# A recurrent layer with a mixture of experts: the second phase's weight sums on VectorE, its additions in DMAs, and a strided down projection

## The chip, the cores and the metric

The kernel runs on one core of one Trainium2 chip. Its engines work side by side and wait for each other through semaphores: TensorE (PE in the profile; its weight loads are PEld), VectorE (DVE), ScalarE (ACT), GpSimd (POOL) and SyncE (SP). SyncE and GpSimd also issue the transfers (DMAs). The metric is the time of one execution on the device in microseconds (us); lower is better. The kernel before takes 4173.52 us (median of 3 runs, 4172.38 to 4174.35).

## What is computed

Eight sequences of 1024 tokens, 512 numbers each (8192 tokens in all), in f32. `_L0_attn_ref` is a gated recurrence with an output projection, `_L0_ffn_ref` a mixture of 32 experts, of which each token uses the best one, beside a shared expert:

```python
x = L0_attn_x
xn = _layernorm(x, axis=-1)
s = _L0_attn_ref(xn, W1, b1, W2, b2, init_h)   # ... out_h @ W2 + b2
g = _silu(_L0_ffn_ref(xn, gate_w, ...))        # shared_out + routed_out
x = x + s * g
```

For a routed token, scaled by its gate's sigmoid, the expert computes `silu(x @ gate) * (x @ up) @ down`; gate and up are 512 x 1024 per expert, down is 1024 x 512.

## The kernel before

**First phase.** 16 chunks of 512 tokens. For each chunk the input projections of the recurrence and of the shared expert are computed, in a seven-product form of block multiplication (Strassen-Winograd: the products P1 to P7 of sums of blocks, in place of eight plain products). The order of all engines is written out by hand in slots. Beside it, one chunk later, `project_out` (from L1166) computes the two output projections of a chunk, called halves: half 0 is `out_h @ W2`, half 1 the shared expert's down projection. Each half has seven products of 8 matmul calls in two PSUM banks, `chain` and `side`. Copies on ScalarE (L1180, L1209, L1217) and additions on VectorE (L1203, L1214) and GpSimd (L1210) bring them into two SBUF tiles, which `out_store` (L1161) writes to `rec2`, a table in device memory with three parts per token: x (copied there by `keep`, L598), the recurrence's output, and the shared expert's output. The normalized, scaled tokens go to `rec1`. The router's choice becomes lists of tokens per expert.

**Second phase.** The experts are taken in order of their number of tokens; the place e has room for `WIDTHS[e]` tokens (376 down to 224), what does not fit goes to a loop at the end (none does here). A `Chunk` is one expert with its tokens, in up to three tiles of 128. Its first stage (gate and up) runs in `strassen` for the places 1 to 27 (width 240 and more) and in `plain` for 0 and 28 to 31. `strassen` has four steps p of seven products each: P1, P5, P2, P6, a down group, P3, P7, a down group, P4. A down group (`down`, L307) multiplies one block of 128 hidden rows by the down weights into four PSUM accumulators; each f32 matmul call shows as two matmuls in the profile, so a group is eight. Down groups run behind: the last two of an expert run in step 0 of the next one. Results of a product are taken from PSUM by ScalarE copies (L384) and VectorE additions (L396, L404 and L406); SiLU on ScalarE and products on VectorE (L408, L413, L416) give the hidden rows. P7 and P4 share a bank: L406 must have read it before P4 is added into it.

The sums of weight blocks that the seven products need are made in `weight_sum` (L213), for each half q of an expert's columns: S3 and S1 on GpSimd (L219, L221), S2 and S4 on VectorE (L223, L225). Each works on 128 x 1024 numbers.

**From the accumulators to the output.** After an expert's last down group, four VectorE transposes in 32 x 32 blocks (L330) read the accumulators into `yT`. `store` writes it to a buffer in device memory by four DMAs on SP (L431), `fetch` reads it back as rows of tokens by up to three DMAs on SP (L440). `gather_rest` (L269) brings the tokens' three parts from `rec2`. Then, for each tile t: `bias` adds b2 (L470), `sums` adds the expert's result to the shared one (L460), `silu` on ScalarE (L465), `finish` multiplies by the recurrence's output and adds x (L478, L479) and scatters the rows to the output by an indirect DMA on GpSimd (L480). The last expert (`direct`) has no store and fetch; TensorE transposes its result (L453).

**The order.** Nothing schedules the second phase: instructions stand on each engine in the order of the calls. A loop (from L1633) puts steps into lists, `between[j]` for the hidden block j of 8; those of an even j run after P6 and the first down group of step p = j / 2, those of an odd j at the end of the step. GpSimd's and SP's queues also work in order: an instruction that waits holds what stands behind it. `alloc2` (L504) sets how many buffers a kind of tile has.

Of the kernel before, what the change touches and what calls it, by code (L numbers as in the profile page):

```python
# [17 lines left out]
P = 128  # L18
# [16 lines left out]
def tile_kernel(  # L35
# [70 lines left out]
    rec1 = dram.tile([N + 1, H], FP, name="rec1")  # L106
    rec2 = dram.tile([N + 1, 3 * H], FP, name="rec2")

# [62 lines left out]
    class Chunk:  # L171
# [41 lines left out]
        def weight_sum(self, q, name):  # L213
            if name == "S3":
                self.sm.append(self.alloc([P, 3, 2 * KQ, QW // 2], "sm", f"{self.name}_sm{q}"))
            s = self.sm[q].rearrange("p s c (b f) -> p s c b f", f=P)
            A11, A12, A21, A22 = (self.quarter(q, a, m) for m in range(2) for a in range(2))
            if name == "S3":
                nc.gpsimd.tensor_tensor(s[:, 1], A11, A21, ALU.subtract)  # L219
            elif name == "S1":  # L220
                nc.gpsimd.tensor_tensor(A21, A21, A22, ALU.add)  # L221
            elif name == "S2":
                nc.vector.tensor_tensor(s[:, 0], A21, A11, ALU.subtract)  # L223
            else:
                nc.vector.tensor_tensor(s[:, 2], A12, s[:, 0], ALU.subtract)  # L225
# [39 lines left out]
        def gather_rest(self):  # L265
            self.rest = []
            for t, n in self.tiles:
                r = self.alloc([P, 3 * H], "rest", f"{self.name}_rest{t}")
# [38 lines left out]
        def down(self, j, h):  # L307
            W = self.width
            for m in range(KH):
                nc.tensor.matmul(  # L310
                    accs[m][:, :W], lhsT=self.wd[:, j, m * P : (m + 1) * P], rhs=h[:, :W],
                    start=(j == 0), stop=(j == NI - 1),
                )
            if j == NI - 1:
                self.evict()

        def evict(self):
            W = self.width
            if self.direct:
                self.yT = self.alloc([P, KH, C], "yT", f"{self.name}_yT")  # L320
                for m in range(KH):
                    if m % 2:
                        nc.vector.tensor_copy(self.yT[:, m, :W], accs[m][:, :W])
                    else:
                        nc.scalar.copy(self.yT[:, m, :W], accs[m][:, :W])
                return
            nb = -(-W // BL)
            self.yT = self.alloc([P, C // BL, KH, BL], "yT", f"{self.name}_yT")
            for m in range(KH):
                nc.vector.transpose(  # L330
                    self.yT[:, :nb, m, :],
                    accs[m][:, : nb * BL].rearrange("p (b c) -> p b c", c=BL),
                )
# [91 lines left out]
        def store(self):  # L425
# [4 lines left out]
            for a in range(NA):  # L430
                nc.sync.dma_start(  # L431
                    out=rows[a, :, :nb, :],
                    in_=self.yT[a * BL : (a + 1) * BL, :nb].rearrange("p b m r -> p b (m r)"),
                )

        def fetch(self):
            rows, self.y = self.y, []
            for t, n in self.tiles:
                y = self.alloc([P, H], "y", f"{self.name}_y{t}")
                nc.sync.dma_start(out=y[:n, :], in_=rows[t * P : t * P + n, :])  # L440
                self.y.append(y)

        def sums(self, t):
# [3 lines left out]
            n = self.tiles[t][1]  # L447
            name, alloc, r = self.name, self.alloc, self.rest[t]
            z = r[:n, 2 * H :]
            if self.direct:  # L450
                y = bank(f"{name}_tb{t}")
                for m in range(KH):
                    nc.tensor.transpose(  # L453
                        y[:n, m * P : (m + 1) * P], self.yT[:, m, t * P : t * P + n], ident
                    )
                nc.vector.tensor_tensor(z, y[:n, :], z, ALU.add)
            else:
                zv = z.rearrange("p (m a r) -> p m a r", a=NA, r=BL)
                y = self.y[t][:n, :].rearrange("p (a m r) -> p m a r", a=NA, r=BL)
                nc.vector.tensor_tensor(zv, y, zv, ALU.add)  # L460

        def silu(self, t):
            if t < len(self.tiles):
                z = self.rest[t][: self.tiles[t][1], 2 * H :]
                nc.scalar.activation(z, z, AF.Silu)  # L465

        def bias(self, t):
            if t < len(self.tiles):
                n, r = self.tiles[t][1], self.rest[t]
                nc.vector.tensor_tensor(r[:n, H : 2 * H], r[:n, H : 2 * H], b2b[:n, :], ALU.add)  # L470

        def finish(self, t):

            if t >= len(self.tiles):
                return
            n, col, r = self.tiles[t][1], self.cols(t), self.rest[t]
            o = r[:n, H : 2 * H]
            nc.vector.tensor_tensor(o, o, r[:n, 2 * H :], ALU.mult)  # L478
            nc.vector.tensor_tensor(o, o, r[:n, :H], ALU.add)  # L479
            store = nc.gpsimd.indirect_dma_start(  # L480
                out=of[:, :], out_offset=bass.IndirectOffsetOnAxis(ap=col[:n, :], axis=0),
                in_=o, in_offset=None, bounds_check=N - 1, oob_is_err=False,
            )

# [82 lines left out]
    class Prep:  # L567
# [173 lines left out]
    def zero_rows():  # L741
# [5 lines left out]
        nc.gpsimd.dma_start(out=rec1[N : N + 1, :], in_=zrow)  # L747
        for q in range(3):
            nc.gpsimd.dma_start(out=rec2[N : N + 1, q * H : (q + 1) * H], in_=zrow)
# [411 lines left out]
    def out_store(c, half, m, o):  # L1161
        i = (c * NT + 2 * m) * P
        rows = rec2[i : i + 2 * P, (half + 1) * H : (half + 2) * H]
        nc.sync.dma_start(out=rows.rearrange("(q p) f -> p q f", p=P), in_=o)

    def project_out():  # L1166

        for n, u in enumerate(units):
# [8 lines left out]

            def evict(name, ps):
                t = part[name] = op.tile([P, 2, HC], FP, tag="e" + name[0], name=f"{name}_{n}")
                nc.scalar.copy(t, ps)  # L1180

            for name in UNIT:
                w = out_w.pop((u, name))
                ps = side if name in ("P2", "P5", "P3") else chain
                for q in range(2):
                    for p in range(NP):
# [12 lines left out]
                        if q == 1 and p == NP - 1:  # L1199
                            if name == "P1":  # L1200
                                evict("a1", ps)
                            elif name == "P2":
                                nc.vector.tensor_tensor(o[0][:, :, :HC], ps, part["a1"], ALU.add)  # L1203
                            elif name == "P6":
                                evict("a2", ps)
                            elif name == "P5":
                                evict("b5", ps)
                            elif name == "P7":
# [7 lines left out]
                            else:  # L1216
                                nc.scalar.copy(o[1][:, :, :HC], ps)  # L1217
                                at(now + 2, out_store, c, half, 1, o[1])
# [407 lines left out]
    with ExitStack() as c3:  # L1626
# [6 lines left out]
        for e, chunk in enumerate(chunks):  # L1633
            between = {j: [] for j in range(NI)}
            ahead = chunks[e + 1] if e + 1 < E else None
            if chunk.split:
                for j, name in ((0, "S3"), (0, "S1"), (2, "S2"), (3, "S4")):
                    between[j].append(lambda name=name: chunk.weight_sum(1, name))
            if e > 1:
                between[0].append(lambda: chunks[e - 2].finish(2))  # L1640
            if e:
                before = chunks[e - 1]
                between[1] += [before.store, before.fetch]
                for t in range(CT):
                    between[3].append(lambda t=t: before.bias(t))
# [22 lines left out]
            if e == E - 1:  # L1668
                between[7].append(lambda: before.finish(2))
                for t in range(CT):  # L1670
                    between[6].append(lambda t=t: chunk.bias(t))
            chunk.compute(pend, between)
# [9 lines left out]
    with tc.tile_pool(name="wo", bufs=3) as wo, tc.tile_pool(name="so", bufs=3) as so:  # L1682
# [4 lines left out]
        with tc.For_i(0, n, 1) as i:  # L1687
# [22 lines left out]
            for t in range(CT):  # L1710
                chunk.bias(t)
                chunk.sums(t)
# [34 lines left out]
```

## Time and profile before

| | us |
|---|---|
| median of 3 runs | 4173.52 |
| the profiled execution | 4176.65 |
| its span, first to last instruction | 4174.5 |
| first phase (to the first expert's matmul) | 2796 |
| second phase (to the last down matmul) | 1359 |
| PE busy | 4112.1 (99%) |
| DVE busy | 2371.7 (57%) |
| ACT busy | 2151.8 (52%) |
| POOL busy | 1428.3 (34%) |

The groups of instructions that the change touches, with count and mean duration:

| line, engine | what | count | mean |
|---|---|---|---|
| L219, POOL | weight sum S3 | 54 | 2367 ns |
| L221, POOL | weight sum S1 | 54 | 2400 ns |
| L223, L225, DVE | weight sums S2, S4 | 54 each | 1222, 1218 ns |
| L470, DVE | bias, tiles of 128 tokens | 54 | 679 ns |
| L460, DVE | result added, tiles of 128 | 53 | 678 ns |
| L478, L479, DVE | product, x added, tiles of 128 | 54 each | 665, 692 ns |
| L310, PE | down matmuls | 2048 | 396 ns |
| L480, POOL | scatters to the output | 84 | 1202 ns |

A bar of a matmul includes the time in which its results leave the array, so bars overlap; how far apart they start tells the rate. The times in a timeline are counted from the start of the span. "idle before" names what an engine waited for.

### The profile page before, as it was taken

The numbers are of one execution on the slowest core, as the hardware profiler recorded it, in microseconds if no ns is written. First come the engines' busy times: TensorE is split into PE (matmuls) and PEld (weight loads), VectorE is DVE, ScalarE is ACT, GpSimd is POOL, SyncE is SP. The second block draws the span as 40 slices with busy tenths as digits, with TensorE's granted clock in tenths as the row PEclk, the third lists the DMA queues.
The fourth block names the chain that finished last, engine by engine and source line by source line (L and its number), as shares of the span: only waits on it lengthen the run. The fifth ranks groups of instructions, "written<-read, shape, count | busy, mean of one in ns | idle before, by whom it ended". The sixth has DMA issues, their size and how long they took to land. (4 is left out here: it accounts for less than half of the span.)

```text
span 4174.5 us, 60006 instructions
## 1 busy us (share of the span) xinstructions
PE 4112.1 (99%) x21515; PEld 3637.9 (87%) x21515; DVE 2371.7 (57%) x3760; ACT 2151.8 (52%) x4095; POOL 1428.3 (34%) x1310
## 2 busy tenths in 40 slices
PE   7999999999999999999999999999999999999998
PEld 5788888888888888888888888877889999899998
DVE  6655544554545545455455555434676777777742
ACT  5667666766767667666676666631222222222211
POOL 5222111221122212212222113643556656565531
PEclk9999999999999999999999999999999999999999
DMA  7666666666666666657666665575667777677784
GB/s 255 234 223 219 212 220 204 217 222 215 220 206 202 229 220 216 215 198 232 211 216 215 209 211 190 181 245 179 222 224 248 245 245 251 240 256 252 256 271 145
DMA packets 567694, 926.13 MB, mean 222 GB/s; under 512 B 41469, under 2 KB 328093, under 8 KB 567394
## 3 DMA queue, kind: packets, MB, share of 16 engines
q1 hardware_dynamic: 539810, 832.29, 60.4%
q0 software_dynamic: 27584, 89.98, 6.5%
q8 instruction: 172, 2.82, 0.3%
q14 instruction: 128, 1.05, 0.1%
HBM read 805.27 MB, written 134.92 MB: 225 GB/s over the span
## 5 line engine op out<-in xcount | busy, mean ns | idle before, releaser
L894 PE MATMUL b<-t,sums 128*128 128x256 f32 x2536 | 652.2, 380 | 3.4 <-ACT u L908 1.8
L1191 PE MATMUL u<-wP,s 128*128 128x256 f32 x2032 | 596.3, 379 | 2.8 <-issue 2.8
L894 PEld LDWEIGHTS b<-t,sums 128*128 128x128 f32 x2536 | 480.7, 190 | 71.7 <-ACT u L908 3.0
L310 PE MATMUL acc<-e_h,e_wd 128*128 128x296 f32 (+15 forms) x2048 | 518.0, 396 | 0.0
L1191 PEld LDWEIGHTS u<-wP,s 128*128 128x128 f32 x2032 | 385.7, 190 | 57.2 <-issue 5.0
L310 PEld LDWEIGHTS acc<-e_h,e_wd 128*128 128x128 f32 x2048 | 374.2, 190 | 67.0
L894 PE MATMUL c<-xnT,sums 128*128 128x256 f32 x1268 | 327.0, 380 | 13.0 <-ACT p L908 11.6
L894 PE MATMUL c<-t,sums 128*128 128x256 f32 x1268 | 326.5, 380 | 4.2 <-ACT a L908 4.2
L894 PE MATMUL b<-xnT,nat 128*128 128x256 f32 x1268 | 326.3, 380 | 0.0
L894 PE MATMUL a<-xnT,nat 128*128 128x256 f32 x1268 | 325.7, 379 | 0.3
L894 PE MATMUL b<-t,nat 128*128 128x256 f32 x1268 | 325.4, 379 | 0.0
L259 POOL DMA_INDIRECT e_xs<-rec,fours x276 | 278.8, 1010 | 94.0 <-issue 81.6
L894 PEld LDWEIGHTS c<-xnT,sums 128*128 128x128 f32 x1268 | 240.5, 190 | 48.9 <-issue 9.3
L894 PEld LDWEIGHTS c<-t,sums 128*128 128x128 f32 x1268 | 241.2, 190 | 37.7 <-issue 4.9
L910 ACT ACTIVATE u<-b,vec 128x256 f32<-128x256 f32 x378 | 180.5, 478 | 178.1 <-PE b L894 178.1
L894 PEld LDWEIGHTS b<-xnT,nat 128*128 128x128 f32 x1268 | 241.5, 190 | 33.5 <-issue 0.5
L894 PEld LDWEIGHTS a<-xnT,nat 128*128 128x128 f32 x1268 | 240.6, 190 | 34.0 <-ACT c L908 1.5
L894 PEld LDWEIGHTS b<-t,nat 128*128 128x128 f32 x1268 | 241.1, 190 | 32.9
L480 POOL DMA_INDIRECT out_dram<-e_rest,idx x84 | 100.9, 1202 | 455.4 <-DVE e_rest L479 425.2
L972 DVE TENSOR_TENSOR d<-d,m 128x1024 f32<-128x1024 f32 x64 | 87.5, 1367 | 255.7 <-ACT m L968 255.7
L1191 PE MATMUL u<-wP,h 128*128 128x256 f32 x768 | 225.2, 379 | 0.0
L1191 PE MATMUL u<-wP,sh 128*128 128x256 f32 x720 | 215.6, 381 | 0.0
(288 smaller groups left out, 7998.2 us busy)
## 6 DMA issues: line engine op xcount, KB each, us to landing
sums<-sdram SPq DMA_DIRECT2D x300, 512.0 KB, 4.7
nat<-in_L_attn_W_dram SPq DMA_DIRECT2D x192, 512.0 KB, 4.3
e_w<-L_ffn_routed_gate_w_dram SPq DMA_DIRECT2D x128, 512.0 KB, 9.8
e_w<-n_L_ffn_routed_up_w_dram SPq DMA_DIRECT2D x128, 512.0 KB, 11.8
e_wd<-L_ffn_routed_down_w_dram SPq DMA_DIRECT2D x32, 2048.0 KB, 8.6
wP<-tdram SPq DMA_DIRECT2D x127, 512.0 KB, 3.7
nat<-L_ffn_shared_gate_w_dram SPq DMA_DIRECT2D x64, 512.0 KB, 4.4
nat<-n_L_ffn_shared_up_w_dram SPq DMA_DIRECT2D x64, 512.0 KB, 4.1
```

Of the source, the lines that this page charges most:

```text
L259: nc.gpsimd.indirect_dma_start(out=r[:, b, :], out_offset=None, in_=rec1.rearrange("n (a d) -> (n a) d", a=NA), in_offset=bass.IndirectOff ...
L310: nc.tensor.matmul(accs[m][:, :W], lhsT=self.wd[:, j, m * P : (m + 1) * P], rhs=h[:, :W], start=(j == 0), stop=(j == NI - 1),)
L480: store = nc.gpsimd.indirect_dma_start(out=of[:, :], out_offset=bass.IndirectOffsetOnAxis(ap=col[:n, :], axis=0), in_=o, in_offset=None, b ...
L894: nc.tensor.matmul(ps, lhsT=lhs[:, k, :], rhs=rhs[:, k, :], start=(new and k == 0), stop=(k == KQ - 1),  skip_group_check=True,)
L910: nc.scalar.activation(o, ps, AF.Identity, bias=bias(n, block))
L972: nc.vector.tensor_tensor(d, d, self.li, ALU.subtract)
L1191: nc.tensor.matmul(ps[:, q, :], lhsT=lhs[:, q * P : (q + 1) * P], rhs=w[:, p, :],  start=(q == 0 and p == 0 and name in ("P1", "P2", "P5") ...
```

## The change

It has five parts, all but one of them in the second phase.

- The weight sums S3 and S1 move from GpSimd to VectorE, and their places in the order move: for the expert that follows, S3 at j = 4, S1 at j = 5, S2 and S4 at j = 7; for the second half of the current one, S3 and S1 at j = 0, S2 and S4 at j = 2.
- The down weights of accumulator m are every fourth column from m on, where they were a block of 128 columns. `yT` holds the four numbers of a token's row next to each other, so the transposes write at a step of four numbers, and the rows in device memory have their natural order.
- `fetch` goes. `sums` is a DMA on GpSimd that adds the stored rows onto the gathered ones in SBUF. SiLU and `finish` come later in the order.
- x goes to the output itself in the first phase (`keep`), `rec2` has two parts, and the scatter in `finish` adds onto the output's rows; VectorE's addition of x goes.
- b2 is added in the first phase: four of half 0's copies on ScalarE become VectorE additions of b2. The step `bias` goes.

```diff
-    rec2 = dram.tile([N + 1, 3 * H], FP, name="rec2")
+    rec2 = dram.tile([N + 1, 2 * H], FP, name="rec2")
...
             if name == "S3":
-                nc.gpsimd.tensor_tensor(s[:, 1], A11, A21, ALU.subtract)
+                nc.vector.tensor_tensor(s[:, 1], A11, A21, ALU.subtract)
             elif name == "S1":
-                nc.gpsimd.tensor_tensor(A21, A21, A22, ALU.add)
+                nc.vector.tensor_tensor(A21, A21, A22, ALU.add)
...
         def down(self, j, h):
             W = self.width
+            wd = self.wd[:, j, :].rearrange("p (q m) -> p m q", m=KH)
             for m in range(KH):
                 nc.tensor.matmul(
-                    accs[m][:, :W], lhsT=self.wd[:, j, m * P : (m + 1) * P], rhs=h[:, :W],
+                    accs[m][:, :W], lhsT=wd[:, m], rhs=h[:, :W],
...
-            self.yT = self.alloc([P, C // BL, KH, BL], "yT", f"{self.name}_yT")
+            self.yT = self.alloc([P, C // BL, BL, KH], "yT", f"{self.name}_yT")
             for m in range(KH):
                 nc.vector.transpose(
-                    self.yT[:, :nb, m, :],
+                    self.yT[:, :nb, :, m],
...
-        def fetch(self):
-            rows, self.y = self.y, []
-            for t, n in self.tiles:
-                y = self.alloc([P, H], "y", f"{self.name}_y{t}")
-                nc.sync.dma_start(out=y[:n, :], in_=rows[t * P : t * P + n, :])
-                self.y.append(y)
...
+            z = self.rest[t][:n, H:]
+            if not self.direct:
+                nc.gpsimd.dma_start(
+                    out=z, in_=self.y[t * P : t * P + n, :], accum_op=ALU.add
+                )
+                return
+            y = bank(f"{self.name}_tb{t}")
+            yv = y.rearrange("p (q m) -> p m q", m=KH)
+            for m in range(KH):
+                nc.tensor.transpose(yv[:n, m], self.yT[:, m, t * P : t * P + n], ident)
+            nc.vector.tensor_tensor(z, y[:n, :], z, ALU.add)
...
-            o = r[:n, H : 2 * H]
-            nc.vector.tensor_tensor(o, o, r[:n, 2 * H :], ALU.mult)
-            nc.vector.tensor_tensor(o, o, r[:n, :H], ALU.add)
-            store = nc.gpsimd.indirect_dma_start(
+            o = r[:n, :H]
+            nc.vector.tensor_tensor(o, o, r[:n, H:], ALU.mult)
+            nc.gpsimd.indirect_dma_start(
...
+                compute_op=ALU.add,
...
-            "xs": 4, "xsT": 2, "sig": 2, "h": 4, "y": 2, "yT": 1, "rest": CT + 2,
+            "xs": 4, "xsT": 2, "sig": 2, "h": 4, "yT": 1, "rest": 2 * CT,
...
-            nc.sync.dma_start(out=rec2[rows, :H], in_=xf[rows, :])
+            nc.sync.dma_start(out=of[rows, :], in_=xf[rows, :])
...
-            def evict(name, ps):
+            def copy(o, ps, m):
+                if half:
+                    nc.scalar.copy(o, ps)
+                else:
+                    bias = b2b[:, m * HC : (m + 1) * HC].unsqueeze(1).to_broadcast([P, 2, HC])
+                    nc.vector.tensor_tensor(o, ps, bias, ALU.add)
+
+            def evict(name, ps, m):
                 t = part[name] = op.tile([P, 2, HC], FP, tag="e" + name[0], name=f"{name}_{n}")
-                nc.scalar.copy(t, ps)
+                copy(t, ps, m)
...
-                for j, name in ((0, "S3"), (0, "S1"), (2, "S2"), (3, "S4")):
+                for j, name in ((0, "S3"), (0, "S1"), (2, "S2"), (2, "S4")):
...
-                        (before.sums, (3, 3, 4)), (before.silu, (4, 4, 5)), (before.finish, (5, 7, 8))
+                        (before.sums, (3, 3, 4)), (before.silu, (5, 5, 6)), (before.finish, (7, 7, 8))
...
-                    between[4] += [lambda n=n: ahead.weight_sum(0, n) for n in ("S3", "S1")]
+                    for j, name in ((4, "S3"), (5, "S1"), (7, "S2"), (7, "S4")):
+                        between[j].append(lambda name=name: ahead.weight_sum(0, name))
                     between[6].insert(1, ahead.row_sums)
-                    between[7] = [
-                        lambda n=n: ahead.weight_sum(0, n) for n in ("S2", "S4")
-                    ] + between[7]
```

The copies of half 0 that become additions of b2 are those of P1, P6, P5 and P4; P7's stays on ScalarE, since the tile of P5 that is added to it has b2 already. `zero_rows` clears two parts of the table's last row in place of three.

More of the change, by code (lines that the diff above doesn't have):

```diff
@@ L267, in gather_rest @@
             for t, n in self.tiles:
-                r = self.alloc([P, 3 * H], "rest", f"{self.name}_rest{t}")
+                r = self.alloc([P, 2 * H], "rest", f"{self.name}_rest{t}")
                 nc.gpsimd.indirect_dma_start(
@@ L432, in store @@
                     out=rows[a, :, :nb, :],
-                    in_=self.yT[a * BL : (a + 1) * BL, :nb].rearrange("p b m r -> p b (m r)"),
+                    in_=self.yT[a * BL : (a + 1) * BL, :nb].rearrange("p b r m -> p b (r m)"),
                 )
-        def fetch(self):
-            rows, self.y = self.y, []
-            for t, n in self.tiles:
-                y = self.alloc([P, H], "y", f"{self.name}_y{t}")
-                nc.sync.dma_start(out=y[:n, :], in_=rows[t * P : t * P + n, :])
-                self.y.append(y)
         def sums(self, t):
@@ L447, in sums @@
             n = self.tiles[t][1]
[L448 to L460, printed above, removed]
+            z = self.rest[t][:n, H:]
[9 more added lines that the diff above has]
+            nc.vector.tensor_tensor(z, y[:n, :], z, ALU.add)
         def silu(self, t):
             if t < len(self.tiles):
-                z = self.rest[t][: self.tiles[t][1], 2 * H :]
+                z = self.rest[t][: self.tiles[t][1], H:]
                 nc.scalar.activation(z, z, AF.Silu)
[L467 to L470, printed above, removed]
         def finish(self, t):
@@ L747, in zero_rows @@
         nc.gpsimd.dma_start(out=rec1[N : N + 1, :], in_=zrow)
-        for q in range(3):
+        for q in range(2):
             nc.gpsimd.dma_start(out=rec2[N : N + 1, q * H : (q + 1) * H], in_=zrow)
@@ L1162, in out_store @@
         i = (c * NT + 2 * m) * P
-        rows = rec2[i : i + 2 * P, (half + 1) * H : (half + 2) * H]
+        rows = rec2[i : i + 2 * P, half * H : (half + 1) * H]
         nc.sync.dma_start(out=rows.rearrange("(q p) f -> p q f", p=P), in_=o)
@@ L1200, in project_out @@
                             if name == "P1":
-                                evict("a1", ps)
+                                evict("a1", ps, 0)
                             elif name == "P2":
@@ L1204, in project_out @@
                             elif name == "P6":
-                                evict("a2", ps)
+                                evict("a2", ps, 1)
                             elif name == "P5":
-                                evict("b5", ps)
+                                evict("b5", ps, 1)
                             elif name == "P7":
@@ L1216, in project_out @@
                             else:
-                                nc.scalar.copy(o[1][:, :, :HC], ps)
+                                copy(o[1][:, :, :HC], ps, 0)
                                 at(now + 2, out_store, c, half, 1, o[1])
@@ L1642, in tile_kernel @@
                 before = chunks[e - 1]
-                between[1] += [before.store, before.fetch]
+                between[1].append(before.store)
                 for t in range(CT):
-                    between[3].append(lambda t=t: before.bias(t))
                     for what, k in (
-                        (before.sums, (3, 3, 4)), (before.silu, (4, 4, 5)), (before.finish, (5, 7, 8))
+                        (before.sums, (3, 3, 4)), (before.silu, (5, 5, 6)), (before.finish, (7, 7, 8))
                     ):
@@ L1669, in tile_kernel @@
                 between[7].append(lambda: before.finish(2))
-                for t in range(CT):
-                    between[6].append(lambda t=t: chunk.bias(t))
             chunk.compute(pend, between)
@@ L1710, in tile_kernel @@
             for t in range(CT):
-                chunk.bias(t)
                 chunk.sums(t)
```

## The prediction

> **What bounds the kernel now.** I read the busy time of each engine by stage first, then TensorE's waits in the second phase, then the timeline around one of them, and last the weight loads.
>
> ```profile
> core 0: us, PE busy (x) PEld busy (x) DVE busy (x) ACT busy (x) POOL busy (x), PEclk, DMA share, GB/s
> 25.00:350.00 325.00, 305.62 (x1362) 254.52 (x1359) 209.18 (x329) 221.92 (x397) 116.39 (x115) 0.99 0.70 234
> 2100.00:2450.00 350.00, 350.00 (x1633) 306.15 (x1632) 180.45 (x267) 238.22 (x429) 75.49 (x83) 1.00 0.67 218
> 2796.00:4155.00 1359.00, 1349.73 (x8741) 1239.96 (x8739) 878.67 (x1441) 304.62 (x774) 718.71 (x547) 1.00 0.71 237
> 4155.00:4174.50 19.50, 1.12 (x8) 0.65 (x6) 4.44 (x7) 1.26 (x2) 1.93 (x2) 0.58 0.06 22
> ```
>
> TensorE is the bound at a full clock. Of its 62.4 us without a matmul (4174.5 - 4112.1), 30.5 lie before 350 us, where the change has nothing, 18.4 in the tail, 4.2 at the phases' border and 9.3 in the second phase. The second phase has one wait on TensorE, seven times:
>
> ```profile
> PE e_b L375 <- DVE e_low L406: 9.0, 7, 1.7
> ```
>
> One of the seven, in the third step (p = 2) of an expert of width 264:
>
> ```profile
> 3588.76 2.40 POOL L219 TENSOR_TENSOR e_sm<-e_w 128x1024 f32<-128x1024 f32 x1
> 3588.82 2.64 DVE L408 TENSOR_TENSOR e_h<-e_sig,e_top 128x264 f32<-128x264 f32 x1 [0.15 <-ACT e_sig L407]
> ...
> 3591.24 2.44 POOL L221 TENSOR_TENSOR e_w<-e_w 128x1024 f32<-128x1024 f32 x1
> 3591.38 2.45 DVE L413 TENSOR_TENSOR e_h<-e_sig1l,e_low 128x132 f32<-128x132 f32 x1
> ...
> 3593.96 1.21 DVE L225 TENSOR_TENSOR e_sm<-e_w,e_sm 128x1024 f32<-128x1024 f32 x1
> 3595.09 0.68 DVE L470 TENSOR_TENSOR e_rest<-e_rest,b2b 128x512 f32<-128x512 f32 x1
> ...
> 3598.10 0.41 DVE L396 TENSOR_TENSOR e_top<-e_a,e_s 128x264 f32<-128x264 f32 x1
> ...
> 3600.36 0.41 DVE L406 TENSOR_TENSOR e_low<-e_b,e_s 128x264 f32<-128x264 f32 x1
> ...
> 3600.82 1.17 PE L375 MATMUL e_b<-e_ts,e_w 128*128 128x132 f32 x8 [1.69 <-DVE e_low L406]
> ```
>
> While GpSimd runs a weight sum (2.40, 2.44 us), a VectorE product with two SBUF inputs stretches to the same length (2.64 and 2.45, against 0.43 and 0.29 in the next step). VectorE enters p = 2 late, has L225 and all bias and result additions ahead of it, and L406 comes after P4 could have started in the bank that L406 reads.
>
> The bars hide a little: groups of eight that last 1.06 start 0.90 apart, so each gap is 0.16 longer than shown: 9.0 + 7 x 0.16 = 10.1 us. L225 also ends late for P3 (0.2 us here), whose loads sat idle 1.8 us more than P4's do without L406 (10.8 against 23.4 - 14.4). I take 12 us in all. A bound: matmuls start 2W/2.4 + 2.5 ns apart (229 for W = 272), 111.7 for the narrow ones, which gives 1345.5 us for the second phase against 1358.5 from its first matmul to its last down one. So 13.0 us is the most that VectorE's relief can bring.
>
> **Weight sums to VectorE, additions off it.** GpSimd loses 54 x 2.37 + 54 x 2.40 = 257 us. VectorE gains 108 sums at L223's 1.22 (132 us) and loses 84 bias additions at 0.68, 82 result additions at 0.68 and 84 additions of x at 0.69 (171 us), besides the stretched products. In p = 2 L225 and the additions (3593.96 to 3598.10) go, and one sum (1.13 from start to start) comes behind L396; L404 and L406 then wait for the matmuls alone. The fullest place becomes p = 0: from the end of the last expert's P4 VectorE runs L416 (0.65 with its wait), two sums (2.3), two products of finish (1.2), L396 (0.35), two sums (2.3), a third finish (0.6), L404 and L406 (0.8): 8.2 us. P4 of p = 0 may start 9.1 us after that end (3578.86 - 3569.80). So L406 is hidden with 0.9 us to spare; past that, each us costs 27 us, one per split expert. Behind it stand L408, L413 and the down products. Gain -12, bounds -13 and -10.
>
> **Every fourth column.** The 2048 loads of L310 now step 16 bytes. No such load is in the trace for a plain f32 matmul; the transposes of L286 load rows at that step, those of L663 contiguous ones:
>
> ```profile
> L310 PEld LDWEIGHTS acc<-e_h,e_wd x2048: 190/190/192, 2811.3 to 4154.4; 128*128 128x128 f32 x187
> L286 PEld LDWEIGHTS e_tp<-ident,e_xs x12: 195/212/219, 2784.4 to 2785.8; 128*128 128x128 f32 x8, 120*128 120x128 f32 x4
> L663 PEld LDWEIGHTS lgt<-ident,lgT x64: 139/141/143, 27.4 to 2486.8; 128*128 128x128 f32 x64
> ```
>
> A strided load lasts 71 ns longer, but twelve of L286 issue in 1.43 us, 119 apart, against 110 for L663. A down matmul gives its successor's load 189 ns (W = 224) to 316 (W = 376), so a load paced at 119 to 127 is hidden inside the down groups. It shows only where a narrow product's matmul (112 to 149 ns) precedes the first down load: 8 times in 27 experts, 216 times 0 to 15 ns: 0.7 to 1.8 us. I take +1.5. The other end: if the 71 ns come on top of 111.7 (183 apart), the 216 places cost 13.4 us; at twice 119 (238 apart), 25 us there and 29 inside the down groups of the narrow experts: 55 us. The nearest row issues at 119, so I take the small end.
>
> The Trainium skill, page SBUF — State Buffer, section "Door 1: The DMA port swizzle", speaks against the edit: SBUF has 16-byte lines, and full rate wants two hits or more in each; a step of four f32 hits each line once. If that halved the load rate, 111.7 would become 223 and the edit would cost some 36 us; by the row it costs 1.5. The trace's 119 is no halving of the plain f32 load, but it is of a transpose's load, which may read less per column.
>
> **Transposed results.** L330 now writes at a 16-byte step. L294, which reads at one, takes 1.97 ns an element from start to start, L330 1.42. If writing costs the same, four transposes grow by 0.6 us, bounds 0 and 1.2. Behind them stand L413, L416 and L396, which is due 3.9 us after the last down group ends and is reached after 1.63 + 0.6 + 0.6 = 2.8; the accumulators are next written five products after it (4.5 us). So nothing, and past that 31 us for each us.
>
> **Additions by DMA.** 82 fetches leave SP's queue (which stood waiting 140 us for the stored results) and 82 accumulating DMAs join GpSimd's, about 1 us of issue each, less than the 257 us that left. No row shows an accumulating DMA. Bounds: a plain fetch lands in 2.9 us, a gather of rest in 8.5, a scatter in 5.2. In the build order a scatter waits for the one before it, and the accumulations follow on the same queue; ScalarE's SiLU waits for them, and ScalarE's copies for the next P6 stand behind it. In the expert above, scatters would start at 3572, 3578 and 3583, the accumulations at 3586 when the stored results are down, landing by 3594. SiLU is due at 3600 and starts to hurt at 3601.5. Cost 0 while landings stay under about twice these; at two and a half times, the third scatter of 19 experts pushes them to about 3608, 6 us late, 115 us in all. I take 0, since scatter and fetch are the nearest rows and hold a factor of two.
>
> The Trainium skill, page Collectives: The Full Stack, section "The bandwidth ceiling: the fold count and why AG ≠ RS ≠ AR", says that an add in the DMA needs two reads and ran at half the rate. With that factor the sum stays as it is, with nothing in hand; with the row's plain scatter there are some 7 us in hand.
>
> **First phase.** Of 16 chunks' rnn half, four copies each (64 x 0.586) go from ScalarE to VectorE at L1203's 0.69, 44 us over 2620 us where VectorE is half idle. Their banks are next needed one product (3.5 us alone, about 12 interleaved) later. 0, bounds 0 and +2.
>
> **Tail.** Two additions go (0.6 each between the last down matmul and the last scatter), eight transposes write PSUM strided (1.41 us now), two scatters land one after the other with a read more. -1.2 to +4; I take +0.5.
>
> **Sum.** -12 + 1.5 + 0 + 0 + 0 + 0.5 = -10.0 on 4176.65 us (span 4174.5): 4166.6. The median of the runs is 3.1 lower than that execution: 4173.5 - 10.0 = 4163.5 us. The bounds give -13 + 0.7 - 1.2 = -13.5 and -10 + 1.8 + 2 + 4 = -2.2: 4160 to 4171.
>
> **Rivals.**
> 1. The load's latency shows at each change of stream (183 apart). For it: the 71 ns in the rows, and product matmuls only 112 apart. Against: 119 in L286. 4173.5 - 12 + 13.4 + 0.5 = 4175.4, no change.
> 2. Slower: strided loads of plain f32 matmuls read each 16-byte step twice and bound the down groups, at L310. They outweigh the gain from about 180 ns a load (13.4 us at 183), and at 238 they cost 55 us: 4173.5 - 12 + 55 + 0.5 = 4217; halfway between, 4196. For it: a plain load lasts 190 where a transpose's lasts 141. Against: a second read could find its 16 bytes still at hand, since L286's rate is no worse than one step a ns.
> 3. Accumulating DMAs land late and ScalarE stands behind SiLU: from two and a half times the plain landings, 4173.5 - 10 + 115 = about 4280.
>
> **How the numbers follow.** 0.2% is 8.3 us (below 4165.2), about what a measurement of this kernel can tell from no change. Forecast 0.60: its gain passes 8.3 us unless the tail or the first phase take their upper ends, so faster 0.45, same 0.15. Rival 1: 0.12 (same 0.08, slower 0.04). Rival 2: 0.17, rival 3: 0.11, both slower. Together faster 0.45, same 0.23, slower 0.32. The forecast's own range is 4160 to 4171; the runs' spread of 1 us below it, rival 1 and the lower half of rival 2 bring 0.80: 4159 to 4200.
>
> **What would show it.** Right: no wait of TensorE on L406 in p = 2, VectorE products at 0.3 to 0.5 us throughout, eight down matmuls still 1.83 us apart at W = 272, SiLU waiting for no DMA. Wrong: L310's matmuls further apart than 2W/2.4 + 2.5 ns, or a longer gap ahead of their first; a wait of TensorE on ScalarE's copies behind SiLU; a new wait on L406 in p = 0.

## The result and the profile after

The changed kernel takes 4225.84 us (median of 4 runs, 4224.64 to 4228.22) beside 4173.94 for the kernel before: a ratio of 1.0126, 95% interval 1.0108 to 1.0143. The prediction said 4163.5, with a range from 4159 to 4200. The profiled execution took 4226.55 us, its span is 4224.48, where it was 4174.54: 49.9 longer (the medians differ by 51.9). In the changed file the lines of the second phase from `down` on stand one further (L310 is L311, L375 is L376, L406 is L407); the scatter is L466.

First the busy times of the page of after, and the stretch from the first expert's matmul to the last down matmul (columns as before: length, PE, PEld, DVE, ACT, POOL, clock, DMA share, GB/s):

```profile
PE 4162.4 (99%) x21515; PEld 3765.1 (89%) x21515; DVE 2282.0 (54%) x3682; ACT 2113.9 (50%) x4031; POOL 1276.4 (30%) x1283
```

```profile
2795.00:4203.00 1408.00, 1400.42 (x8746) 1367.72 (x8745) 744.08 (x1303) 297.43 (x774) 581.48 (x520) 1.00 0.74 216
```

VectorE and GpSimd have less to do, as planned (744 us where there were 879, 581 where there were 719), and the stretch has grown from 1359 to about 1407. The weight loads are what grew: PEld is busy for 1368 us of it, where it was 1240. The loads of L311 and TensorE's waits in the second phase of after:

```profile
L311 PEld LDWEIGHTS acc<-e_h,e_wd x2048: 307/316/332, 2810.3 to 4201.5; 128*128 128x128 f32 x187
```

```profile
PE e_b L376 <- DVE e_sm L223: 6.9, 18, 0.4
PE e_tb L451 <- DVE e_yT L324: 0.2, 1, 0.2
```

A load of every fourth column lasts 316 ns, where a load of a block lasted 190. The seven waits on L406 (9.0 us) are gone, and eighteen short ones have come, for a weight sum. What the loads do to a down group shows in TensorE's timeline at a width of 240, first in the trace of before, then of after:

```profile
3953.32 1.79 PE L310 MATMUL acc<-e_h,e_wd 128*128 128x240 f32 x8
3954.95 1.05 PE L375 MATMUL e_b<-e_ts,e_w 128*128 128x120 f32 x8
```

```profile
4002.89 2.13 PE L311 MATMUL acc<-e_h,e_wd 128*128 128x240 f32 x8
...
4004.85 1.05 PE L376 MATMUL e_c<-e_xsT,e_sm 128*128 128x120 f32 x8
```

From the start of the eight to the start of the next group it was 1.63 us, 204 ns for each matmul, and is 1.96. The 1.96 is uneven: in the trace of after, the second of the eight starts 0.33 us after the first, and from there on they start 233 ns apart. (The first expectation below takes the mean, 245 ns, for the rate of the loads; it is 233, with one longer step at the front.) No wait is written beside the group, since the engine is never idle: a slower stream looks busy. That is why the busy share says 99% in both profiles.

The eighteen new waits look like this (timeline of after, VectorE's and TensorE's lines):

```profile
3999.36 1.28 DVE L465 TENSOR_TENSOR e_rest<-e_rest 128x512 f32<-128x512 f32 x2
...
4000.57 1.22 DVE L223 TENSOR_TENSOR e_sm<-e_w 128x1024 f32<-128x1024 f32 x1
...
4001.93 1.12 PE L376 MATMUL e_b<-e_ts,e_sm 128*128 128x120 f32 x8 [0.42 <-DVE e_sm L223]
```

P6 of step 0 multiplies by S2 (L223). The change puts S2 behind the two products of `finish` (L465), which now come at j = 7 too; S2 ends at 4001.79 and P6 starts at 4001.93.

To split the 49.9 us, I set the groups of eight matmuls of two traces side by side, one by one (all 1092 groups of the second phase stand in one order in them), and added up by how much each group starts later after the group ahead of it. The third column compares before with the run that has a step of two and S2 in its old place (described below), which has neither flaw (P4 is a step's last product, P1 the first of the next step):

| ahead of | after against step of two | before against step of two |
|---|---|---|
| P3, P4, the next plain group or the last transposes, that is behind a down group | 18.1 + 18.1 + 9.8 + 1.1 = 47.1 | 10.5 (P4, by L406) |
| P6 and the down group behind it | 11.37 + 1.86 = 13.2 | 0.0 |
| P1, behind P4 | 0.0 | 1.5 |
| all of the second phase | 60.3 | 12.2 |

So the second phase grew by 60.3 - 12.2 = 48.1 us: 47.1 for the loads, 13.2 for S2, and 12.2 came back from L406. The first phase is 1.0 us shorter (first expert's matmul at 2795.4, before 2796.4), the tail from the last down matmul to the end 2.8 longer (22.4, before 19.6). Together 49.9. The 1.0 is no gain of the change: in the runs below, the first phase lasts 2792.7 us in one that has it as before and in one that has it as changed, and 2798.1 in another of the changed ones.

The 47.1 us have two parts of about one size. Where a down group follows a narrow product, its second matmul starts 329 to 376 ns after the first, where with a step of two it starts 218 to 296 ns after it: 22.9 us over 216 groups. The rest, 24.2 us, is lost at the other matmuls, 233 ns apart, in the experts of width 272 and less.

### The profile page after: what moved, and what is told of

The parts are those of the page before. It is cut to its first block, busy times and chain, and to the rows that moved or that the text cites. A ratio compares the mean times of both kernels' runs of the same rounds, so it can differ in the third digit from the quotient of the medians.

```text
span 4224.5 us, 59547 instructions
## 1 busy us (share of the span) xinstructions
PE 4162.4 (99%) x21515; PEld 3765.1 (89%) x21515; DVE 2282.0 (54%) x3682; ACT 2113.9 (50%) x4031; POOL 1276.4 (30%) x1283
## 5 line engine op out<-in xcount | busy, mean ns | idle before, releaser
L311 PE MATMUL acc<-e_h,e_wd 128*128 128x296 f32 (+15 forms) x2048 | 565.8, 419 | 0.0
L311 PEld LDWEIGHTS acc<-e_h,e_wd 128*128 128x128 f32 x2048 | 515.0, 318 | 1.3
L466 POOL DMA_INDIRECT out_dram<-e_rest,idx x84 | 140.6, 1673 | 618.9 <-DVE e_rest L465 302.6
```

The lines of the kernel that those rows point to most:

```text
L311: nc.tensor.matmul(accs[m][:, :W], lhsT=wd[:, m], rhs=h[:, :W], start=(j == 0), stop=(j == NI - 1),)
L466: nc.gpsimd.indirect_dma_start(out=of[:, :], out_offset=bass.IndirectOffsetOnAxis(ap=col[:n, :], axis=0), in_=o, in_offset=None, bounds_ch ...
```

## The experiments

**Blocks of columns in the changed kernel** and, the other way round, **every fourth column in the kernel before**. Each touches one operand:

```diff
-                    accs[m][:, :W], lhsT=wd[:, m], rhs=h[:, :W],
+                    accs[m][:, :W], lhsT=self.wd[:, j, m * P : (m + 1) * P], rhs=h[:, :W],
```

> The changed kernel with the down weights in blocks of 128 columns again, all else as changed; the result's columns then come out in another order than the reference's. Theory (a load at a 16-byte step issues only every 245 ns, 2048 times): its weight loads last 190 ns instead of 316, eight down matmuls at W = 240 start 1.63 us after one another's first instead of 1.96, and the time falls by 48 to 55 us from 4225.8 to 4171 to 4178. Of the rest there stays -13 (no wait on L406), +10 (18 waits of P6 on the sum S2, 0.42 + 0.16 each), +3 in the tail, -1 in the first phase. Rival (accumulating DMAs or VectorE's new order cost the time): it stays above 4200.

> The kernel before with one edit, every fourth column of the down weights (its result's columns are in another order than the reference's). Theory: the loads alone cost 48 to 55 us: 4174 + 51 = 4225 (4222 to 4230), about the changed kernel's time, with 316 ns a load; the seven waits on L406 shrink, since the down group between P7 and P4 is longer by 0.14 to 0.33 us, so up to 3 us less. Rival (the loads cost only what they show at the change of stream, 13 us, and the rest is the new order): about 4187.

Measured: 4180.68 us (4177.01 to 4182.37) for the first, a ratio of 1.0012 to before (1.0002 to 1.0022); 4214.37 (4212.19 to 4216.03) for the second, 1.0095 (1.0078 to 1.0112). So the one operand carries nearly all of the loss: the step alone takes the kernel before from 4175.78 (its median beside these runs) up by 38.6 us, and taking it out of the changed kernel brings 45.2 (47.0 when each is set against the kernel before that ran beside it). In the second run the same table of groups, against before, gives 17.98 + 11.77 + 9.82 + 1.06 = 40.6 us behind down groups; the 11.8 is 18 less what L406 gives back, since slower down groups leave VectorE more time (waits of 3.3 us in 4, before 9.0 in 7). I had allowed 3 us for that, and the run shows 6 to 7. The first run came out 3 us above the upper end of what was expected: its waits on S2 were priced at 10 us there and cost 13.2 (see the run with S2 first), and the kernel before beside it took 1.8 us more than in the first measurement:

```profile
PE e_b L376 <- DVE e_sm L223: 6.9, 18, 0.5
```

**Steps of one, two, four and eight numbers side by side.** In each down group the four accumulators load at a step of 4, 8, 16 and 32 bytes, out of two rows of weights:

```diff
+            two = self.wd[:, at0 : at0 + 2, :].rearrange("p j f -> p (j f)")
+            nc.tensor.matmul(accs[0][:, :W], lhsT=two[:, 0:P], rhs=r, **to)
+            w2 = two[:, 0 : 2 * P].rearrange("p (q s) -> p s q", s=2)
+            nc.tensor.matmul(accs[1][:, :W], lhsT=w2[:, 0], rhs=r, **to)
...
```

> The kernel before with the four down matmuls of a group reading weights at steps of 1, 2, 4 and 8 numbers (4, 8, 16 and 32 bytes), each on a line of its own; the columns multiplied are not those of the reference. Theory (each of the two beats of an f32 column pays for a 16-byte line that no neighbour shares): steps 1 and 2 alike, 190 ns, or step 2 little longer; steps 4 and 8 alike, about 316. Rival (cost grows with the step): 8 longer than 4, and 2 halfway between 1 and 4, about 250.

Measured: 4185.17 us, a single run. The loads, by line, in the order of the steps (count, then shortest, median and longest in ns):

```profile
L313 PEld LDWEIGHTS acc<-e_h,e_wd x512: 190/190/209, 2807.8 to 4161.6; 128*128 128x128 f32 x171
L315 PEld LDWEIGHTS acc<-e_h,e_wd x512: 195/197/197, 2808.4 to 4162.0; 128*128 128x128 f32 x171
L317 PEld LDWEIGHTS acc<-e_h,e_wd x512: 307/308/332, 2809.0 to 4162.4; 128*128 128x128 f32 x171
L319 PEld LDWEIGHTS acc<-e_h,e_wd x512: 312/328/338, 2809.7 to 4162.9; 128*128 128x128 f32 x171
```

It isn't the step as such: two numbers in each 16 bytes cost 7 ns, one number costs 118, and doubling the step once more 20.

**S2 and S4 first at j = 7**, as in the kernel before, on top of the run with blocks:

```diff
-                    for j, name in ((4, "S3"), (5, "S1"), (7, "S2"), (7, "S4")):
+                    for j, name in ((4, "S3"), (5, "S1")):
...
+                    between[7] = [
+                        lambda n=n: ahead.weight_sum(0, n) for n in ("S2", "S4")
+                    ] + between[7]
```

> As the changed kernel with blocks of columns (the result's columns in another order), and the two sums S2 and S4 for the next expert put ahead of the products of finish on VectorE at j = 7. Theory (P6 of step 0 waits for S2 because two products of 0.6 us stand ahead of it): the 18 waits of 0.42 us go, -10 us against the kernel with blocks alone, 4161 to 4168. Rival (VectorE is full there whatever the order): the waits move to L407 or the next product and the time stays within 3 us of it.

Measured: 4166.25 us (4163.76 to 4168.93), 0.9979 of before (0.9969 to 0.9988), 14.4 less than the run with blocks. TensorE has no wait on VectorE left in the second phase. The groups of the two runs differ ahead of P6 and the down group behind it by 11.35 + 1.85 = 13.2 us and nowhere else, though the waits printed come to 6.9: the bar of a matmul hides part of a gap.

**The output's columns in their order, with blocks.** The transposes write contiguously, and `store` puts the rows in order by 16 DMAs with pieces of 128 bytes in place of four with 512:

```diff
+                for m in range(KH):
+                    nc.sync.dma_start(
+                        out=rows[a, m, :, :nb, :], in_=self.yT[a * BL : (a + 1) * BL, :nb, m, :]
+                    )
```

> The version with blocks of columns and S2 and S4 first at j = 7 (4166.25), with the output's columns in their own order: yT as in the kernel before, written to device memory in 16 transfers of 128-byte pieces in place of four of 512-byte ones. Theory: the transposes are short again (0.45 us in place of 0.68) and VectorE isn't the bound, so the time is 4164 to 4168, if the 16 smaller transfers land before the accumulating DMAs need them. Rival: small pieces hold up SP's queue (weights and gathers behind it) and the accumulations, and TensorE waits for more: over 4175.

This run gave 4254.11 us, on a chip where the kernel before itself took 4392.61; its time can't stand beside the others', and the question of the small pieces stays open. Its transposes last 442 ns (median), as expected. Three of the four kernels below were first run on that chip too, with these expectations:

> The version with S2 and S4 first at j = 7, but the down weights at a step of two numbers (accumulators 0 and 1 take even and odd columns of the first 256, 2 and 3 of the last): yT holds two numbers of a row side by side, and eight transfers of 256-byte pieces store it. Theory (a load costs more once a 16-byte line holds just one of its numbers): loads last 197 ns, the down groups of the narrow experts keep 1.63 us from start to start, and the time is 4164 to 4169, below both kernels. Rival (any step costs in a stream of such loads, four in a row, though it didn't in one of a mixed stream): over 4185.

> The run with a step of two, and in the last expert the finish of the one before it at j = 6 in place of 7 and 8. Theory: the tail's growth (19.5 to 22.4 us) is the chain of four scatters, each of which waits for the one before it to land; with the two of the expert before starting 5 to 10 us earlier, the tail shrinks by 2 to 5 us: 4160 to 4166. Rival: the tail is set by the last expert's own transposes, additions and two scatters: within 1 us of the run with a step of two.

> The run with a step of two, and S3 and S1 on GpSimd again (both at j = 0, and at j = 4 for the next expert): the one part of the change that moved weight sums is undone, the additions stay in the DMAs and in the first phase. Theory (VectorE was late at L406 mainly because of the additions ahead of it): no or at most 2 us of waits on L406, within 3 us of the run with a step of two, though VectorE's products stretch to 2.4 us again. Rival (the stretched products made it late): waits of 5 us or more on L406, 4171 to 4178. GpSimd's queue holds its DMA issues behind the sums, so the accumulating ones may land late too: then TensorE waits on ScalarE's copies and the time is above either.

They took 4298.95, 4305.78 and 4424.78 us. All four then ran on another chip, where the kernel before took 4369.55:

> The run with a step of two once more, beside a kernel before that runs at its usual time (the last one stood beside 4393 us, where engines also waited 2 to 6 us at a time for work that had ended). Theory: loads 197 ns, narrow down groups 1.63 us from start to start, no wait of TensorE on VectorE in the second phase: 4164 to 4169. Rival (the eight smaller transfers land the stored results too late, or any step costs in a stream of such loads): over 4176.

> The run with a step of two and, in the last expert, the finish of the one before it at j = 6, once more beside a kernel before at its usual time. Theory (the tail's growth is the chain of four scatters): the tail shrinks by 2 to 5 us against the run with a step of two. Rival (the tail is the last expert's own transposes, additions and two scatters): within 1 us.

> The run with a step of two and S3 and S1 on GpSimd again, once more beside a kernel before at its usual time. Theory (the additions that are gone suffice): at most 2 us of waits on L406, which is L407 here, and within 3 us of the run with a step of two. Rival (the products that stretch beside GpSimd's sums made VectorE late): waits of 5 us or more there, 4171 to 4178; or the accumulating DMAs, issued behind the sums, land too late, and ScalarE's copies hold TensorE.

> The kernel before with S3 and S1 on VectorE at their old places and nothing else changed: the bias, result and x additions stay on VectorE. If the stretched products made VectorE late, the seven waits on L406 (9.0 us) go: 4162 to 4167. If the additions alone did, the 132 us of sums come on top of them: the waits stay or grow, 4173 to 4185. If each was enough to make it late or to relieve it, this run and the one with the sums on both engines are both near 4165.

They took 4269.79, 4265.83, 4420.54 and 4383.90 us there, with stalls of several us that no line explains in all of them, so that none of the three questions could be read from them. The times and the lines below are of a third run of each, a second of the last, beside a kernel before at the usual 4173.91.

**A step of two.** Accumulators 0 and 1 take the even and odd columns of the first 256, 2 and 3 those of the last; S2 and S4 stand first at j = 7; `store` needs eight DMAs with pieces of 256 bytes:

```diff
-            wd = self.wd[:, j, :].rearrange("p (q m) -> p m q", m=KH)
+            wd = self.wd[:, j, :].rearrange("p (s q m) -> p s m q", s=2, m=2)
...
-                    accs[m][:, :W], lhsT=wd[:, m], rhs=h[:, :W],
+                    accs[m][:, :W], lhsT=wd[:, m // 2, m % 2], rhs=h[:, :W],
```

> The run with a step of two a third time, for a chip on which the kernel before takes 4174 to 4176. Theory: loads 197 ns, narrow down groups 1.63 us from start to start, no wait of TensorE on VectorE in the second phase: 4164 to 4169. Rival (the eight smaller transfers land the stored results too late, or any step costs in a stream of such loads): over 4176.

Measured: 4165.50 us (4164.11 to 4167.89), 0.9980 of before (0.9971 to 0.9990). Its loads, and a down group at a width of 240:

```profile
L311 PEld LDWEIGHTS acc<-e_h,e_wd x2048: 195/197/198, 2810.3 to 4141.2; 128*128 128x128 f32 x187
```

```profile
3892.90 1.80 PE L311 MATMUL acc<-e_h,e_wd 128*128 128x240 f32 x8
3894.54 1.05 PE L376 MATMUL e_b<-e_ts,e_w 128*128 128x120 f32 x8
```

1.64 us from start to start, as before. TensorE waits for nothing in the second phase, which takes 1346.2 us from the first expert's matmul to the last expert's transposes, where the kernel before takes 1358.4 and the changed one 1406.5.

**The last scatters earlier.** On top of that, in the last expert, `finish` of the one before it comes at j = 6:

```diff
-                        (before.sums, (3, 3, 4)), (before.silu, (5, 5, 6)), (before.finish, (7, 7, 8))
+                        (before.sums, (3, 3, 4)), (before.silu, (5, 5, 6)),
+                        (before.finish, (6, 6, 6) if e == E - 1 else (7, 7, 8)),
```

> The run with a step of two and, in the last expert, the finish of the one before it at j = 6, for a chip at the usual time. Theory (the tail's growth is the chain of four scatters): 2 to 5 us less than the run with a step of two. Rival (the tail is the last expert's own transposes, additions and two scatters): within 1 us.

Measured: 4161.97 us (4160.71 to 4164.81), 0.9971 of before (0.9960 to 0.9983), 3.5 less than without it (the two tails differ by 4.9 us, the first phases of the two profiled executions by 2.7 the other way). GpSimd's lines of the tail, in after (last down matmul's end at 4202.07, span 4224.5), and in this run (4144.47 and 4163.0):

```profile
4197.86 1.82 POOL L466 DMA_INDIRECT out_dram<-e_rest,idx  x1 [19.51 <-DVE e_rest L465]
4203.89 1.45 POOL L466 DMA_INDIRECT out_dram<-e_rest,idx  x1 [4.21 <-DVE e_rest L452]
4208.94 1.56 POOL L466 DMA_INDIRECT out_dram<-e_rest,idx  x1 [3.60 <-issue]
4214.56 1.43 POOL L466 DMA_INDIRECT out_dram<-e_rest,idx  x1 [4.07 <-issue]
```

```profile
4136.78 1.82 POOL L469 DMA_INDIRECT out_dram<-e_rest,idx  x1 [11.15 <-DVE e_rest L468]
4142.47 1.45 POOL L469 DMA_INDIRECT out_dram<-e_rest,idx  x1 [3.87 <-DMA out_dram<-e_rest,idx]
4147.69 1.56 POOL L469 DMA_INDIRECT out_dram<-e_rest,idx  x1 [3.76 <-DVE e_rest L468]
4153.06 1.43 POOL L469 DMA_INDIRECT out_dram<-e_rest,idx  x1 [3.82 <-issue]
```

Four scatters stand in a chain, 5 to 6 us from one to the next, each waiting for the one before it to land. Most of these lines name something else, but the trace of after has the first three landings at 4203.1, 4208.2 and 4213.8, and the next scatter starts 0.7 to 0.8 us behind each. In after the first starts 4.2 us before the last down matmul ends; here 7.7 before. From that end to the end of the span it is 22.4 us in after, 23.5 in the run with a step of two, and 18.6 here.

**One half of the change without the other.** First S3 and S1 back on GpSimd, on top of the step of two; then S3 and S1 on VectorE in the kernel before, with nothing else changed:

```diff
-                nc.vector.tensor_tensor(s[:, 1], A11, A21, ALU.subtract)
+                nc.gpsimd.tensor_tensor(s[:, 1], A11, A21, ALU.subtract)
...
-                nc.vector.tensor_tensor(A21, A21, A22, ALU.add)
+                nc.gpsimd.tensor_tensor(A21, A21, A22, ALU.add)
```

> The run with a step of two and S3 and S1 on GpSimd again, for a chip at the usual time. Theory (the additions that are gone suffice): at most 2 us of waits on L406, which is L407 here, and within 3 us of the run with a step of two. Rival (the products that stretch beside GpSimd's sums made VectorE late): waits of 5 us or more there, 4171 to 4178; or the accumulating DMAs, issued behind the sums, land too late.

> The kernel before with S3 and S1 on VectorE at their old places and nothing else changed, for a chip at the usual time. If the stretched products made VectorE late, the seven waits on L406 (9.0 us) go: 4162 to 4167. If the additions alone did, the 132 us of sums come on top of them: the waits stay or grow, 4173 to 4185.

Measured: 4264.78 us (4260.36 to 4267.47) for the first, 1.0215 of before (1.0198 to 1.0232); 4176.75 (4175.02 to 4181.01) for the second, 1.0008 (0.9999 to 1.0018). The first misses its theory and the time of its first rival (4171 to 4178); the second lies in the range of its second case (4173 to 4185), in which the waits stay. TensorE's only wait in the second phase of the one, none of it on ScalarE as late accumulations would bring, and its wait on L406 in the other:

```profile
PE e_b L376 <- DVE e_low L407: 64.9, 25, 5.7
```

```profile
PE e_b L375 <- DVE e_low L406: 8.6, 16, 1.0
```

The first is 99 us slower than the run with a step of two, and the main reason is neither of the two that I had named. Its timeline around one wait:

```profile
3113.66 1.58 POOL L469 DMA_INDIRECT out_dram<-e_rest,idx  x1 [6.26 <-DVE e_h L414]
...
3117.88 2.35 POOL L219 TENSOR_TENSOR e_sm<-e_w 128x1024 f32<-128x1024 f32 x1
...
3120.31 2.35 POOL L221 TENSOR_TENSOR e_w<-e_w 128x1024 f32<-128x1024 f32 x1
...
3122.70 1.23 DVE L223 TENSOR_TENSOR e_sm<-e_w 128x1024 f32<-128x1024 f32 x1 [5.99 <-POOL e_w L221]
...
3125.49 0.46 DVE L407 TENSOR_TENSOR e_low<-e_b,e_s 128x304 f32<-128x304 f32 x1
...
3126.00 1.30 PE L376 MATMUL e_b<-e_ts,e_w 128*128 128x152 f32 x8 [2.69 <-DVE e_low L407]
```

GpSimd's queue works in order. The scatter at 3113.66 had waited 6.26 us; its line names a VectorE product, but by the trace's record of landings the scatter before it, issued at 3105.56, landed at 3112.87, and this one waits for that. The sums L219 and L221 stand behind it, and VectorE waits 5.99 us for L221 before it can make S2 (L223); L407 stands behind that, and TensorE waits for L407. VectorE waits so in 26 of the 27 split experts, 122.9 us in all; in the kernel before it waited 15 times for L221, 34.9 us in all. So the sums can't stay on GpSimd behind scatters that wait like this; whether another order on GpSimd would do was not tried.

The second phase is 98.0 us longer than with a step of two: 69.0 us lie ahead of P4, and 28.5 in the four products behind it. After 14 of the 25 waits those products run slowly: after the one that ends at 3841.32, eight narrow matmuls take 1.86 us from start to start in place of 0.89, and the clock granted from 3841.2 to 3842.0 is 0.50. The stretching that I had named as a rival has a share too: in five late experts L225 lasts 4.0 us in place of 1.2 beside a sum on GpSimd, and the waits there are 4.5 to 5.7 us long, where the others reach 3.3.

In the second run the products no longer stretch (L408 lasts at most 525 ns), yet as much waiting is left as before: VectorE has 132 us of sums more and the additions still ahead of L406. Neither half, placed as it was here, gives the gain; both together give it whole.

## Why the prediction was wrong, step by step

**What bounds the kernel.** Right: TensorE at a full clock, and 10 to 13 us to be had behind L406. Before and the run with a step of two differ by 12.2 us in the second phase, where the sum had -12. That the two agree so well is in part luck: of the 12, 10.1 stood ahead of P4, where 10.5 were found, but the 1.8 that the sum added for P3's loads shrinks to 0.1, and 1.5 came back at P1 behind P4, which it had not named.

**Weight sums to VectorE, additions off it.** Right where it was worked out: VectorE's products last 0.3 to 0.5 us (L409 at most 515 ns), and no wait on L406, now L407, is left in p = 0 or elsewhere. But "the fullest place becomes p = 0" was checked against L406 alone. In the list that I added up there ("L416 ..., two sums (2.3), two products of finish (1.2)") the sums come first; in the trace the products do. For L406, behind both, the order is all one; for P6 of the same step, which needs S2, the first of the sums, it isn't. What the sum took as 0 cost 13.2 us.

**Every fourth column.** This is the step that failed: "The nearest row issues at 119, so I take the small end", +1.5 us. The loads cost 47.1 us; the large end of the bounds, "at twice 119 (238 apart)", gave 55 and a time of 4217, and that rival, at a chance of 0.17, is what happened to the loads (the measured 4225.8 has S2's waits besides): they start 233 ns apart, and they cost 22.9 us at the change of stream and 24.2 inside the groups, where the rival had 25 and 29. The row was near in its step and far in its kind. A transpose's load of rows lasts 141 ns contiguous and 212 at a step of four, a plain f32 load 190 and 316: 71 ns more in the one, 126 in the other, and the interval goes from 111.7 to 233 where the transpose's went from 110 to 119. "A second read could find its 16 bytes still at hand" doesn't hold for the plain load.

The Trainium skill, page SBUF — State Buffer, section "Door 1: The DMA port swizzle", says that a read at full rate needs two or more hits in each 16-byte line. This case agrees in kind, and at that border: with two numbers in each 16 bytes a load lasts 197 ns, with one 308. The estimate from a halved rate, 36 us, was nearer than the row's 1.5, and still below 47.1.

**Transposed results.** 676 ns in the median where 450 stood, 0.9 us for four, inside the bounds of 0 and 1.2; TensorE waits for none of them. At a step of two numbers they last 445.

**Additions by DMA.** The 0 is right, one reason for it is not. An accumulating DMA into SBUF lands in 8.6 us (median, longest 11.7), three times the plain fetch's 2.9: the nearest row did not hold within a factor of two. The scatter, which sets when the accumulations can start, takes 6.9 where it took 5.2, and no SiLU waits for a DMA; the closest landing came 0.4 us ahead of its SiLU, the median one 6.1. GpSimd's issues got longer, 1.67 us for a scatter where the mean was 1.20, and are hidden. The Trainium skill, page Collectives: The Full Stack, section "The bandwidth ceiling: the fold count and why AG ≠ RS ≠ AR", has an add in the DMA at half the rate, for large collectives. A landing time, 1.3 times the plain one for the scatter and 3 times for the fetch, is no rate, so no run here shows whether that holds.

**First phase and tail.** 0 against -1.0, which is within what the first phase varies by from run to run. For the tail I took +0.5 within -1.2 to +4, and it is +2.8: I counted the last expert's two scatters, while those of the expert before it, moved to j = 7, stand in the same chain.

**The sum.** -12 + 1.5 + 0 + 0 + 0 + 0.5 = -10 was expected; -12.2 + 47.1 + 13.2 - 1.0 + 2.8 = +49.9 was found, as in the spans. With a step of two and S2 first the change is worth 8 us, and 12 with the tail mended.

## What to carry to other kernels

In these runs a step in the operand of a weight load cost next to nothing as long as two f32 numbers of each 16 bytes were used (7 ns a load), and 118 ns with one: where a layout wants a step of four, split it into two of two. When work is put onto an engine, check every consumer of every instruction that is now ahead of or behind it, in each step, and not only the consumer that waited before; and a price taken from another kind of instruction is one bound, not the middle. An edit of two parts may pay only as a whole, so test the halves before dropping one of them.

## What the runs showed of the hardware

- The price of a strided weight load has a cliff and then a plateau: 190 ns at a step of one number, 197 at two, 308 at four, 328 at eight. At a step of four the loads of a down group issue 233 ns apart, where contiguous ones issue 112 apart. VectorE's transpose of PSUM into SBUF shows the same cliff on the writing side: 450 ns contiguous, 445 at a step of two, 676 at four.
- An accumulating DMA into SBUF lands in 8.6 us, where the plain fetch of the same rows took 2.9 (nine landings seen) and the gather of the same tiles 8.5 before and 7.7 after. Issuing one takes GpSimd 1.47 us.
- On two of the chips the kernel before takes 4370 to 4393 us in place of 4174. The traces taken there have the first phase at its usual length; in the second, engines wait 2 to 6 us at a time for nothing that the trace shows. The step of two is 2.2 to 2.4% ahead of before there, in place of 0.2%. What causes it wasn't tried.
